# Remainders of up to 64 rows of a routed layer, multiplied two experts at a time

## The chip, the core and the metric

The kernel runs on one core of one Trainium2 chip. The core has TensorE (PE in the profile, its weight loads PEld), VectorE (DVE), ScalarE (ACT), GpSimd (POOL) and SyncE (SP, which here mainly issues transfers), each with its own instruction stream, and 16 DMA engines that all queues share. The metric is the device time of one execution in microseconds (us). One profiled execution, with a record of every instruction, stands beside the timed runs.

## The reference, cut to what matters

Four layers follow each other, each added to `x` (3125 rows of 256): an attention over a graph, a layer of 16 experts of which each row uses two, a sum over the graph, and a layer of 8 experts of which each row uses one. The change is in the last one:

```python
H = gelu(xf @ W1 + b1, approximate=False)          # 3125 x 1024
probs = softmax((H @ Wg + bg) / TEMP, axis=-1)     # 3125 x 8
assign = argmax(probs, axis=-1)
for e in range(8):
    y = H @ Wd[e] + bd[e]                          # Wd[e]: 1024 x 256
    out = out + where((assign == e)[:, None], probs[:, e:e + 1] * y, 0.0)
x = x + out
```

Only the product with the chosen expert's `Wd[e]` is needed for a row. Which rows choose which expert is known only when the kernel runs.

## The kernel before, in words

The last layer is `routed_top1`. Its first part goes through the nodes in chunks of 512: hidden values `H`, the gate's product, the choice, and for every row its place among the rows of its expert. Each row (1024 hidden values, 256 values of `x`, its number and its probability, 1282 floats in all) is written to the DRAM table `rows` by an indirect transfer, the rows of expert `e` one behind another from `e * 3200` on. A matrix product then gives `total`, the rows of each expert.

From `total` some twenty small VectorE operations on a single partition make the `table` of slots. A slot is 128 rows of one expert. `table[0]` holds the slot's expert and `table[1]` its first row in `rows`. An expert with n rows has ceil(n / 128) slots; its last slot can be nearly empty. All weights `Wd` were loaded into `t_wd` (`d` in the code) before, 8 copies of 1 MB (line 1600). While the table is made, `keep_warm` lets TensorE run matmuls whose results nobody reads (line 558).

The second part, `slots`, runs 30 slots (`USUAL`), one after another, for all inputs. If there are more (`rest` is 1), the conditional part at the end runs those up to `SLOTS` with fewer buffers. One slot is:

- SP reads the expert and the first row from `table` and issues the copy of 128 rows into `hs` (641 KB, line 1044) and of the expert's bias (line 1046). There are four buffers of `hs`, so the rows of slot s wait until slot s-4 has been finished by VectorE.
- TensorE turns the 128 x 1024 hidden values in eight transposes (`ps_cols`, line 1051), ScalarE copies them to `hsT` (line 1052).
- TensorE reads the expert from `table` too, and multiplies (`multiply`, `ps_y`, line 1024): eight products of 128 x 128 by 128 x 256, each of two instructions in float32. The product of a slot comes after the transposes of the next.
- VectorE adds the bias (line 1027), scales and adds `x` (line 1028) and converts the row numbers (`who`, line 1031). POOL writes the rows of `out` with an indirect transfer (line 1032).

A scheduler sets the order of the instructions on each engine within what the data allow. On SP the order is that of the program in this part.

With the reference's inputs the eight experts have 525, 260, 708, 139, 167, 442, 490 and 394 rows.

Two places outside this part matter below. Each layer of the graph keeps its data in two large blocks of the pool `big`; none is read any more once the first part of `routed_top1` is over. And the layer of 16 experts already multiplies remainders of up to 64 rows in pairs: `first_more` and `second_more` hold the rows of one expert in the lower and of another in the upper half of a tile, fetch both experts' weights (line 817), and multiply each half with its own:

```python
for j in range(nh):
    for half, _, _, o in own:
        nc.tensor.matmul(ps[half], hid[:, j, half], o[:, j], start=(j == 0), stop=(j == nh - 1))   # line 847
```

Of the kernel before, what the change touches and what calls it, by code (L numbers as in the profile page):

```python
# [10 lines left out]
F32 = mybir.dt.float32  # L11
F16 = mybir.dt.float16
BF16 = mybir.dt.bfloat16
I32 = mybir.dt.int32
# [3 lines left out]
OP = mybir.AluOpType  # L18
AX = mybir.AxisListType
# [3 lines left out]
P = 128  # L23
N = 3125
NT = 25
LAST = N - (NT - 1) * P
NP = NT * P
D = 256
# [9 lines left out]
NX0, HID0 = 16, 512  # L38
NX1, HID1 = 8, 1024
# [484 lines left out]
SHARE = P // 2  # L524
SUBS = NX0 * (CAP0 - EACH * P) // SHARE
BETWEEN = 5
CAP1 = 1024
SLOTS = (N + NX1 * (P - 1)) // P
USUAL = 30
ROW0 = D + 2  # L530
ROW1 = HID1 + D + 2
QUAD = 32
# [350 lines left out]
            nc.sync.dma_start(x[:, t:t + n], sums[t * P:(t + n) * P].rearrange("(t p) f -> p t f", p=P))  # L883


def routed_top1(tc, x, xnT, ident, iota, count, weights, rows, out, over):

# [1 line left out]

    nc = tc.nc
    before, every = count
    (a, b1, (g, fold), gb), (d, bd) = weights
    nh = HID1 // P
    with tc.tile_pool(name="u1", bufs=1) as cp:
        first = cp.tile([P, NX1], F32, name="first")
# [8 lines left out]
                                channel_multiplier=-1)  # L906
# [3 lines left out]
        pre = cp.tile([P, NT + 1, NX1], BF16, name="pre")  # L910
        nc.vector.memset(pre[:, 0], 0.0)
        table = cp.tile([1, 2, SLOTS], I32, name="table")
        warm = cp.tile([P, P], F32, name="warm")
        nc.gpsimd.memset(warm, 0.0)
        rest = cp.tile([1, 1], I32, name="rest")
        end = cp.tile([1, 4, 2 * NX1], F32, name="end")
        nc.vector.memset(end, 0.0)
        with tc.tile_pool(name="uh", bufs=2) as hp, tc.tile_pool(name="uw", bufs=2) as wp, \
             tc.tile_pool(name="ur", bufs=6) as rp, \
             tc.tile_pool(name="uph", bufs=2, space=PSUM) as pp, \  # L920
# [66 lines left out]
            keep_warm(nc, tp.tile([P, CHUNK], F32, name="ps_rows"), warm, d[:, 0, 0:2].rearrange("p j f -> p (j f)"), 8)  # L987
            nc.vector.tensor_reduce(over, total, AX.X, OP.max)
            ni = cp.tile([1, NX1], I32, name="n_i")
            nc.vector.tensor_scalar(ni, total, float(P - 1), None, op0=OP.add)  # L990
            nc.vector.tensor_scalar(ni, ni, 7, None, op0=OP.arith_shift_right)

            nc.vector.tensor_copy(end[:, 0, NX1:], ni)
            for j in range(3):
                nc.vector.tensor_tensor(end[:, j + 1, NX1:], end[:, j, NX1:], end[:, j, NX1 - (1 << j):-(1 << j)],
                                        op=OP.add)
            end = end[:, 3, NX1:]
            nc.vector.tensor_scalar(rest, end[:, NX1 - 1:], float(USUAL), None, op0=OP.is_gt)
            slot = cp.tile([1, SLOTS], F32, name="slot")
            nc.gpsimd.iota(slot, pattern=[[1, SLOTS]], base=0, channel_multiplier=0,  # L1000
                           allow_small_or_imprecise_dtypes=True)
# [13 lines left out]

            nc.vector.tensor_scalar(table[:, 1], slot, float(NX1 * NT), float(P), op0=OP.min, op1=OP.mult)

        def slots(which, pools):
            xp, sp, tp, po = pools

            def multiply(hs, hsT, bias, e):
                ps = po.tile([P, D], F32, name="ps_y")
                for j in range(nh):
                    nc.tensor.matmul(ps, hsT[:, j], d[:, ds(e, 1), j, :].rearrange("p o f -> p (o f)"),  # L1024
                                     start=(j == 0), stop=(j == nh - 1))
                y = sp.tile([P, D], F32, name="y")
                nc.vector.tensor_tensor(bias, ps, bias, op=OP.add)
                nc.vector.scalar_tensor_tensor(y, bias, hs[:, HID1 + D + 1:], hs[:, HID1:HID1 + D], op0=OP.mult,
                                               op1=OP.add)
                who = sp.tile([P, 1], I32, name="who")  # L1030
                nc.vector.tensor_copy(who, hs[:, HID1 + D:HID1 + D + 1])
                independent(tc, "out", nc.gpsimd.indirect_dma_start(
                    out=out, out_offset=bass.IndirectOffsetOnAxis(ap=who, axis=0), in_=y, in_offset=None,
                    bounds_check=N - 1, oob_is_err=False))

            ready = None
            for s in which:
                e = nc.values_load(table[0:1, 0, s:s + 1], engines=(mybir.EngineType.PE, mybir.EngineType.SP), min_val=0,
                                   max_val=NX1 - 1, skip_runtime_bounds_check_because="min with the last expert")
                at = nc.values_load(table[0:1, 1, s:s + 1], engines=(mybir.EngineType.SP,), min_val=0,  # L1040
                                    max_val=NX1 * NP, skip_runtime_bounds_check_because="min with the spare tile")
                hs = xp.tile([P, ROW1], F32, name="hs")
                for c, n in ((0, ROW1),) if s else ((0, HID1 // 2), (HID1 // 2, ROW1 - HID1 // 2)):
                    nc.sync.dma_start(hs[:, c:c + n], rows[ds(at, P), c:c + n])
                bias = xp.tile([P, D], F32, name="bias")
                nc.sync.dma_start(bias, bd[ds(e, 1), :].to_broadcast([P, D]))
                hsT = xp.tile([P, nh, P], F32, name="hsT")
                for h in range(0, nh, 4):
                    ps = tp.tile([P, 4, P], F32, name="ps_cols")
                    for j in range(4):  # L1050
                        nc.tensor.transpose(ps[:, j], hs[:, (h + j) * P:(h + j + 1) * P], ident)  # L1051
                    nc.scalar.copy(hsT[:, h:h + 4], ps)  # L1052
                if ready:
                    multiply(*ready)
                ready = hs, hsT, bias, e
            multiply(*ready)

        def pools(stack, bufs):
            return [stack.enter_context(tc.tile_pool(name=name, bufs=b, **kw)) for name, b, kw in (
                ("vx", min(4, bufs), {}), ("vs", bufs, {}), ("vpt", min(4, bufs), dict(space=PSUM)),  # L1060
                ("vpo", min(3, bufs), dict(space=PSUM)))]

        with ExitStack() as stack:
            slots(range(USUAL), pools(stack, 6))
        more = nc.values_load(rest[0:1, 0:1], min_val=0, max_val=1, skip_runtime_bounds_check_because="0 or 1")
        with tc.If(more > 0), ExitStack() as stack:
            slots(range(USUAL, SLOTS), pools(stack, 2))

# [62 lines left out]
def block(big, d=D):  # L1133

    return big.tile([P, NT * ROW], F32, name="big")[:, :NT * d].rearrange("p (t d) -> p t d", d=d)
# [459 lines left out]


def output_weights(nc, cp, wd, bd):
    d = cp.tile([P, NX1, HID1 // P, D], F32, name="t_wd")
    for e in range(NX1):
        nc.sync.dma_start(d[:, e], wd[e].rearrange("(k p) f -> p k f", p=P))  # L1600
    return d, bd


WIN = 5
# [406 lines left out]
@with_exitstack  # L2011
def routed(ctx: ExitStack, tc: tile.TileContext, i: dict, out: bass.AP, over):
    nc = tc.nc
    const = ctx.enter_context(tc.tile_pool(name="const", bufs=1))
    dram = ctx.enter_context(tc.tile_pool(name="dram", bufs=1, space=DRAM))
    ident, eps, iota = constants(tc, const)
    count = counters(tc, const)
    rows0 = dram.tile([NX0 * NP + P, ROW0], F32, name="rows0")
    rows = dram.tile([NX1 * NP + P, ROW1], F32, name="rows1")
    sums = dram.tile([NP + CAP0, D], F32, name="sums0")  # L2020
    layers = [[i[f"L0_gnn_{n}{j}"] for n in ("W", "al", "ar", "b")] for j in (1, 2, 3)]
    big = ctx.enter_context(tc.tile_pool(name="big", bufs=2))
    early = ctx.enter_context(tc.tile_pool(name="early", bufs=1))
    more = early.tile([1, 3, SUBS], I32, name="more")
    with tc.tile_pool(name="counts", bufs=1) as kp:
        counts = kp.tile([P, NT * ((len(GROUPS) - 1) * PAIR + 64)], U8, name="counts")
        x = dense_attention(tc, dram, counts, i["x"], big, ident, eps, layers, i["src"], i["dst"], (rows0, rows),
                            over[:, 3:4], lambda cp: Router(tc, cp, ident, eps, iota, count, rows0, sums,
                                                            i["L0_ffn_gate_w"], i["L0_ffn_gate_b"], more), over[:, 0:1], count)
        with tc.tile_pool(name="s0", bufs=1) as sp:  # L2030
            ws, wm = (sp.tile([P, KD, D], F32, name="s_" + n) for n in "WM")
            hidden = hidden_weights(nc, early, *(i["L1_ffn_" + n] for n in ("W1", "b1", "Wg", "bg")), x[:, 0, 0:1])
            room = block(big).rearrange("p t d -> p (t d)")
            xnT = room.rearrange("p (k n) -> p k n", k=KD)
            routed_experts(tc, x, room, ident, rows0, sums, more, *(i["L0_ffn_" + n] for n in ("w1", "w2", "w3")),
                           lambda behind: [two_halves(nc, to, i["L1_gnn_" + n], behind) for to, n in ((ws, "W"), (wm, "M"))])
            dense_sum(tc, x, xnT, counts, ws, wm, ident, eps, over[:, 2:3])
    late = ctx.enter_context(tc.tile_pool(name="late", bufs=1))
    weights = hidden, output_weights(nc, late, *(i["L1_ffn_" + n] for n in ("Wd", "bd")))
    routed_top1(tc, x, xnT, ident, iota[:, NX0 - NX1:], count, weights, rows, out, over[:, 1:2])  # L2040


def load_nodes(nc, x, x_in, first=0, end=NT):
# [88 lines left out]
```

## Time and profile before

| | |
|---|---|
| three timed runs | 1888.25, 1891.96, 1897.26 us (median 1891.96) |
| the profiled execution | 1840.01 us |
| its span, first to last instruction | 1838.2 us |
| first part of `routed_top1` | from 1551 to 1686 us |
| table and warming matmuls | from 1686 to 1696 us |
| slots | from 1696 to 1829 us |
| rows of a slot (`hs`, 641 KB), issue to landing | 2.6 / 4.3 / 6.5 us (least / median / most) |
| bias of a slot (128 KB), issue to landing | 3.3 / 4.0 / 7.1 us |
| resident `Wd` (1 MB each, 8 in a row), issue to landing | 5.7 / 10.7 / 12.2 us |

The profile has a page and further views. The page gives each engine's busy time and what share of the span that is. The windows give, for a stretch of time, the busy time of each engine with the number of its instructions, the clock granted to TensorE (1.00 is full), the mean busy share of the DMA engines and the rate in GB/s. The timeline lists single instructions or runs of equal ones, with start and duration; at the end of a line, in brackets, stands how long the engine was idle and what ended it. The chain of waits goes back from the last instruction to what released each, and lists its pieces in order of time. "L1044" is line 1044 of the kernel.

### The profile page before, as it was taken

The page shows a single profiled execution, that of the slowest core. Times are in us where ns is not written, and L with a number is a line of the kernel's source. Part 1 is how long each engine was busy: PE and PEld are TensorE (multiplying, and loading weights), DVE is VectorE, ACT ScalarE, POOL GpSimd, SP SyncE. Part 2 cuts the span into 40 slices and gives each one's busy share as a digit, 9 for nine tenths or more (in the row PEclk, how much of TensorE's full clock was granted, in tenths as well). Part 3 has the DMA queues.
Part 4 walks back from the last instruction along what each step waited for, and adds up shares of the span by engine and source line. Part 5 has one row for each costly group of instructions (what it writes and reads, how often), then busy time and mean ns, then how long its engine had stood idle before and what let it go on. Part 6 is the DMA issues. An engine that isn't in the chain of part 4 may idle for free. (4 is left out here: it accounts for less than half of the span.)

```text
span 1838.2 us, 27323 instructions
## 1 busy us (share of the span) xinstructions
PE 1771.2 (96%) x9249; PEld 1389.5 (76%) x9249; DVE 1017.4 (55%) x2865; ACT 725.4 (39%) x2078; POOL 501.5 (27%) x636
## 2 busy tenths in 40 slices
PE   5999999999999999999999799999989999999997
PEld 4788888887887886888888466666668886555886
DVE  6888888875777887777777422222262222233221
ACT  3767667671111111222222211111148998444221
POOL 5210110000677774223322233333200000222221
PEclk9999999999999999999999899999999999999999
DMA  4111213757333332211111576776330002624664
GB/s 118 33 48 47 67 64 139 298 236 312 80 93 95 98 93 78 62 46 40 40 44 37 178 196 196 204 217 168 66 82 1 1 1 74 225 115 166 215 203 127
DMA packets 118370, 211.50 MB, mean 115 GB/s; under 512 B 14843, under 2 KB 80929, under 8 KB 118184
## 3 DMA queue, kind: packets, MB, share of 16 engines
q1 hardware_dynamic: 78228, 130.30, 20.9%
q0 software_dynamic: 24848, 56.84, 11.8%
q10 hardware_dynamic: 15138, 22.44, 3.7%
q8 instruction: 79, 1.29, 0.3%
q14 instruction: 77, 0.63, 0.1%
HBM read 118.61 MB, written 93.00 MB: 115 GB/s over the span
## 5 line engine op out<-in xcount | busy, mean ns | idle before, releaser
L1391 PE MATMUL acc<-big,pm 128*128 128x257 f32 x3400 | 787.7, 383 | 8.9 <-DVE pm L1388 8.9
L1391 PEld LDWEIGHTS acc<-big,pm 128*128 128x128 f32 x3400 | 628.6, 190 | 99.4 <-DVE pm L1388 15.4
L1388 DVE SCALAR_TENSOR_TENSOR pm<-tau,big,counts 128x256 f32<-128x256 f32 x850 | 398.3, 487 | 99.9 <-PE acc L1391 96.0
L1933 POOL DMA_INDIRECT apart_row<-apart_rows,apart_who x172 | 186.7, 1085 | 62.6 <-issue 39.3
L775 PE MATMUL ps_h<-xsT,w 128*128 128x384 f32 x512 | 168.4, 487 | 0.6 <-ACT xsT L751 0.6
L1543 PE MATMUL acc<-msg,cr 128*128 128x512 f32 (+1 forms) x625 | 157.9, 403 | 0.0
L775 PEld LDWEIGHTS ps_h<-xsT,w 128*128 128x128 f32 x512 | 96.7, 190 | 66.9 <-issue 1.9
L1543 PEld LDWEIGHTS acc<-msg,cr 128*128 128x128 f32 (+1 forms) x625 | 114.7, 185 | 29.2 <-ACT cr L1539 1.2
L1539 ACT ACTIVATE cr<-counts 128x256 fp32r<-128x256 uint8 (+1 forms) x325 | 130.6, 402 | 14.2 <-PE acc L1543 7.0
L1799 ACT CAST counts<-acc_c 128x500 uint8<-128x500 f32 (+1 forms) x155 | 95.9, 677 | 94.8 <-PE acc_c L1789 94.7
L1024 PE MATMUL ps_y<-t_wd,hsT 128*128 x480 | 108.8, 380 | 0.4 <-ACT hsT L1052 0.4
L1774 DVE TENSOR_TENSOR ohk<-iota_k,key 128x2016 f16<-128x2016 f16 (+1 forms) x79 | 94.6, 1197 | 19.8 <-PE acc_c L1789 19.7
L778 ACT ACTIVATE silu<-ps_h 128x384 f32<-128x384 f32 x64 | 31.4, 490 | 182.2 <-PE ps_h L775 182.1
L795 POOL DMA_INDIRECT sums<-y,who x48 | 74.7, 1556 | 85.9 <-DVE y L793 73.0
L1024 PEld LDWEIGHTS ps_y<-t_wd,hsT 128*128 128x128 f32 x480 | 88.8, 190 | 11.6 <-ACT hsT L1052 0.6
L779 DVE TENSOR_TENSOR hid<-silu,ps_h 128x384 f32<-128x384 f32 x64 | 35.2, 553 | 108.7 <-PE ps_h L775 103.9
L1768 ACT ACTIVATE ohs<-iota_s,low 128x128 f16<-128x128 f16 x286 | 94.1, 400 | 0.0
L930 PE MATMUL ps_H<-big,t_w 128*128 128x512 f32 (+1 forms) x224 | 93.1, 552 | 0.8 <-ACT H L932 0.5
L790 PE MATMUL ps_o<-w,hid 128*128 128x256 f32 x384 | 87.2, 379 | 0.0
L1789 PEld LDWEIGHTS <-ohs 128*128 128x128 f16 x1250 | 77.7, 98 | 10.9
L1789 PE MATMUL acc_c<-ohk,ohs 128*128 128x125 f16 x1250 | 84.5, 218 | 0.0
L1959 DVE SCALAR_TENSOR_TENSOR apart_acc<-apart_row,apart_co,apart_acc 128x257 f32<-128x257 f32 x167 | 80.9, 485 | 1.6
(380 smaller groups left out, 2073.5 us busy)
## 6 DMA issues: line engine op xcount, KB each, us to landing
rows<-empty SPq DMA_DIRECT2D x16, 2564.0 KB, 15.7
w<-in_L_ffn_w_dram ACTq DMA_DIRECT2D x42, 512.0 KB, 4.9
hs<-rows SPq DMA_DIRECT2D x29, 641.0 KB, 4.4
big<-in_L_ffn_w_dram SPq DMA_DIRECT2D x30, 512.0 KB, 9.2
rows<-empty SPq DMA_DIRECT2D x16, 516.0 KB, 4.8
t_wd<-in_L_ffn_Wd_dram SPq DMA_DIRECT2D x8, 1024.0 KB, 10.7
xs<-rows SPq DMA_DIRECT2D x15, 387.0 KB, 3.4
bias<-in_L_ffn_bd_dram SPq DMA_DIRECT2D x30, 128.0 KB, 4.0
```

The costliest lines, as they stand in the source:

```text
L775: nc.tensor.matmul(ps, w[:, k, j * P:(j + 1) * P], xsT[:, k], start=(k == 0), stop=(k == KD - 1))
L930: nc.tensor.matmul(ps[:, :n], a[:, k, j * P:(j + 1) * P], xnT[:, k, c:c + n], start=(k == 0), stop=(k == KD - 1))
L1024: nc.tensor.matmul(ps, hsT[:, j], d[:, ds(e, 1), j, :].rearrange("p o f -> p (o f)"), start=(j == 0), stop=(j == nh - 1))
L1388: nc.vector.scalar_tensor_tensor(pm[:, :n], tau[:, :n], now.rho[:, of:of + 1], edges[:, of, :n], op0=OP.max, op1=OP.mult)
L1391: nc.tensor.matmul(acc[:r, j, :D + 1], pm[:, q:q + r], now.h[:, of, :D + 1], start=(s == 0), stop=(s == NT - 1))
L1539: nc.scalar.activation(cr[:, :n], edges[:, s, :n], AF.Copy, accum_out=seen[:, a * NT + s:a * NT + s + 1])
L1543: nc.tensor.matmul(acc[:r, j].rearrange("p h d -> p (h d)"), cr[:, q:q + r], msg[:, s].rearrange("p h d -> p (h d)"), start=(s == 0), stop ...
L1768: nc.scalar.activation(far[:, i], self.iota_s, AF.Abs, scale=-1.0, bias=self.low32[:, batch, i:i + 1])
L1774: nc.vector.tensor_tensor(to[:, i:tiles].rearrange("p t (x u) -> p t x u", u=2), iota.rearrange("p (x u) -> p x u", u=2)[:, None].to_broad ...
L1789: nc.tensor.matmul(acc[:, u], ohs[:, i], ohk[:, i, :KEYS], start=(t == 0), stop=(t == TW - 1))
L1799: nc.scalar.copy(to[:, :, d0 % PAIR:d0 % PAIR + whole * WIN].rearrange("p s (u d) -> p u s d", u=whole), acc[:, :whole])
L1933: nc.gpsimd.indirect_dma_start(out=row[:, j], out_offset=None, in_=self.table[:, :], in_offset=bass.IndirectOffsetOnAxis(ap=self.who[:, q ...
```

## The change

An expert's last rows no longer fill a slot of 128 if they are 64 or fewer. They become a half. Full slots are now floor((n + 63) / 128) for n rows; an expert with rows beyond these has one half. Two halves, of two experts, make a pair: their rows lie in the lower and the upper 64 partitions of one `hs`, and each half is multiplied with its own expert's weights, 64 rows wide, into its half of one PSUM tile.

24 slots and 3 pairs run for all inputs; 4 more slots and one pair are in the conditional part, which runs if there are more than 24 full slots or more than 6 halves. The table of slots has 28 columns instead of 32. A second table, `ends` (named `ends_table`), holds expert and first row of each half, and is made by further small operations on VectorE.

The pairs come after the slots. Their weights aren't taken from `t_wd`, but fetched from DRAM into two blocks of `big` (three halves of 1 MB in each); TensorE then needs no expert number for them. The fetches are issued on SP, one ahead of the rows of every second slot from slot 6 (`LATER`) on: at slots 6, 8, 10, 12, 14 and 16.

The core of the diff:

```diff
-SLOTS = (N + NX1 * (P - 1)) // P
-USUAL = 30
+SLOTS = (N + NX1 * (P - SHARE - 1)) // P
+USUAL = 24
+PAIRS = NX1 // 2
+USUAL_PAIRS = 3
+LATER = 6
...
-            nc.vector.tensor_scalar(ni, total, float(P - 1), None, op0=OP.add)
+            nc.vector.tensor_scalar(ni, total, float(P - SHARE - 1), None, op0=OP.add)
             nc.vector.tensor_scalar(ni, ni, 7, None, op0=OP.arith_shift_right)
...
+            own = cp.tile([1, NX1], F32, name="own_half")
+            nc.vector.scalar_tensor_tensor(own, whole, float(P), total, op0=OP.mult, op1=OP.is_lt)
+            nc.vector.tensor_copy(last[:, 0, NX1:], own)
...
+            nc.vector.tensor_scalar(many[:, 0:1], end[:, NX1 - 1:], float(USUAL), None, op0=OP.is_gt)
+            nc.vector.tensor_scalar(many[:, 1:2], last[:, NX1 - 1:], float(2 * USUAL_PAIRS), None, op0=OP.is_gt)
+            nc.vector.tensor_tensor(rest, many[:, 0:1], many[:, 1:2], op=OP.max)
...
+        blocks = [block(big, ROW).rearrange("p t d -> p (t d)") for _ in range(2)]
...
                 for j in range(nh):
-                    nc.tensor.matmul(ps, hsT[:, j], d[:, ds(e, 1), j, :].rearrange("p o f -> p (o f)"),
-                                     start=(j == 0), stop=(j == nh - 1))
+                    for part, of in own:
+                        nc.tensor.matmul(ps[part], hsT[:, j, part], of(j), start=(j == 0), stop=(j == nh - 1))
...
+            def halves(k):
+                e = nc.values_load(ends[0:1, 0, k:k + 1], engines=(mybir.EngineType.SP,), min_val=0,
+                                   max_val=NX1 - 1, skip_runtime_bounds_check_because="min with the last expert")
+                to = blocks[k // 3 % 2][:, k % 3 * nh * D:(k % 3 + 1) * nh * D].rearrange("p (j f) -> p j f", f=D)
+                nc.sync.dma_start(to, wd[ds(e, 1)].rearrange("o (k p) f -> p (o k) f", p=P))
+                return e, to
...
+            for s, of, parts in [(s, table, [whole]) for s in which] + \
+                    [(2 * s, ends, [slice(0, SHARE), slice(SHARE, P)]) for s in pairs]:
                 hs = xp.tile([P, ROW1], F32, name="hs")
...
+                soon = [k for k in range(2 * pairs[0], 2 * pairs[-1] + 2) if k not in loaded]
+                if of is table and s >= LATER and s % 2 == 0 and soon:
+                    loaded[soon[0]] = halves(soon[0])
+                for k, part in enumerate(parts):
...
+                    for c, n in ((0, ROW1),) if s or of is ends else ((0, HID1 // 2), (HID1 // 2, ROW1 - HID1 // 2)):
+                        nc.sync.dma_start(hs[part, c:c + n], rows[ds(at, rs), c:c + n])
+                    nc.sync.dma_start(bias[part], bd[ds(e, 1), :].to_broadcast([rs, D]))
...
-            slots(range(USUAL), pools(stack, 6))
+            slots(range(USUAL), range(USUAL_PAIRS), pools(stack, 6))
...
-            slots(range(USUAL, SLOTS), pools(stack, 2))
+            slots(range(USUAL, SLOTS), range(USUAL_PAIRS, PAIRS), pools(stack, 2))
```

## The prediction

> **What bounds the kernel now.** I read the busy shares and the 40 slices first, then the windows of the last stage, then the chain of waits, then single rows. The page says where the end is set:
>
> ```profile
> PE 1771.2 (96%) x9249; PEld 1389.5 (76%) x9249; DVE 1017.4 (55%) x2865; ACT 725.4 (39%) x2078; POOL 501.5 (27%) x636
> ```
>
> TensorE is busy 96% of the span. A share is an average, so the stage of the change, the output slots, is read alone. It runs from 1696 us to 1829 us (busy time of the engines, granted clock, DMA share, GB/s):
>
> ```profile
> 1700.00:1740.00 40.00, 40.00 (x227) 35.76 (x226) 9.50 (x28) 10.74 (x20) 8.80 (x9) 1.00 0.67 210
> 1740.00:1780.00 40.00, 40.00 (x223) 35.71 (x222) 9.57 (x27) 9.66 (x18) 8.78 (x9) 1.00 0.68 212
> ```
>
> TensorE has no gap here and full clock. Every other engine is under a quarter busy, apart from the weight loads, which run beside the matmuls. The chain of waits gives the beat of a slot:
>
> ```profile
> 1724.51 0.87 PE ps_cols L1051 x8
> 1725.39 3.46 PE ps_y L1024 x16
> 1728.84 0.87 PE ps_cols L1051 x8
> ```
>
> A slot is 0.87 us of transposes and 3.46 us of multiplication, 4.33 us from slot to slot. Nothing else is in the chain, so a slot less is 4.33 us less, as long as rows and weights keep coming in time.
>
> **How many slots go.** The gate of the reference, evaluated on its own inputs, sends 525, 260, 708, 139, 167, 442, 490 and 394 rows to the eight experts. Rounded up to 128 these are 5+3+6+2+2+4+4+4 = 30 slots, all that the kernel before runs. After the change a remainder of up to 64 is a half: 13, 4, 11, 39, 58 and 10 are (experts 0, 1, 3, 4, 5, 7), 68 and 106 are not. So 24 full slots and 6 halves, which is exactly 24 slots and 3 pairs. The flag `rest` stays 0 and the conditional slots are jumped over.
>
> **Removed.** Six slots at 4.33 us: -26.0 us of TensorE time on the path.
>
> **Added on TensorE: three pairs.** A pair has the same 8 transposes (0.87 us) and twice as many matmuls: for each of 8 blocks one with the 64 rows of one half and one with those of the other, each streaming 256 columns. The stage has no such row, but an earlier one of this trace does: line 847 multiplies two halves of 64 rows into the two halves of one PSUM tile in the same way, also with 256 columns. Timeline of that place (start, duration):
>
> ```profile
> 1110.25 1.89 PE L790 MATMUL ps_o<-w,hid 128*128 128x256 f32 x8
> 1112.07 1.95 PE L847 MATMUL ps_o<-big,silu 128*64 128x256 f32 x16
> 1113.95 0.59 PE L775 MATMUL ps_h<-xsT,w 128*128 128x384 f32 x1
> ```
>
> Eight full-width instructions took 1.82 us from start to start, the sixteen half-width ones 1.88 us. Two halves run side by side for the price of one. At 3.46/16 = 0.216 us, eight instructions are 1.73 us, so going into the half-width form cost 0.09 us and coming out 0.15 us. In the changed program the 96 half-width matmul instructions of the pairs stand in three runs, parted by transposes: three entries and two exits before the end, 0.6 us. Three pairs: 3 x 4.33 + 0.6 = +13.6 us.
>
> A rule of the Trainium skill speaks against this. TensorE: Matmul & The Clock Gate, Part 3, "The mechanism", says that a weight load overlaps a running matmul only where the row groups differ, and both halves here use all 128 rows. By the rule each couple would pay two loads (0.137 us each, median of line 847) and 0.216 us of streaming: 0.49 us, 16 couples 7.8 us, three pairs 3 x (0.87 + 7.8) = 26.1 us, and the change would gain nothing (-26.0 + 26.1). The rows disagree: 16 loads of 137 ns, 2.2 us in all, went by within 1.88 us that also held their matmuls. I take the row.
>
> **Added on SP: the fetched weights.** Six copies of 1 MB of `Wd` into free blocks of `big`, one ahead of the rows of slots 6, 8, 10, 12, 14 and 16, each with a load of its expert number from `ends`. SP needs about 0.7 us for that: 0.38 us to issue (median of line 817, the same kind of copy) and 0.3 us for the number. Before the stage settles SP passes a slot in 1.66 us (issues of `hs` at 1694.17 and 1695.83); afterwards it waits for a free row buffer, so 0.7 us vanishes in the wait. Behind SP stand the rows `hs` and the bias of the next slot. What can hurt is the transfer:
>
> ```profile
> 1703.98 0.33 SPq L1044 DMA_DIRECT2D hs<-rows  x1
> 1708.17 0.15 DVE L1031 CAST who<-hs 128x1 int32<-128x1 f32 x1
> 1711.15 0.90 PEld L1051 LDWEIGHTS ps_cols<-ident,hs 128*128 128x128 f32 x7
> ```
>
> The rows of slot 4 are issued at 1703.98, their first reader `who` has them at 1708.17, and TensorE takes them at 1711.15: 7.2 us from issue to need, 4.2 us used, 3.0 us to spare. The fetch of the resident weights shows the full rate (same columns as above):
>
> ```profile
> 1556.00:1561.00 5.00, 4.82 (x12) 2.20 (x12) 0.00 (x0) 2.41 (x5) 0.00 (x0) 1.00 1.09 354
> 1561.00:1566.00 5.00, 5.00 (x13) 2.28 (x12) 0.00 (x0) 2.06 (x3) 0.00 (x0) 1.00 1.09 348
> ```
>
> At 350 GB/s 1 MB takes 3.0 us. Two slots now move 8.66 us x 211 GB/s = 1.83 MB; with 1.05 MB more it is 333 GB/s, 95% of the full rate, for the 12 slots that fetch. That fits, with little left. My estimate of the landing: the copy is issued some 2.4 us before the next rows, so about 1.5 us of it is still ahead of them: 4.2 + 1.5 = 5.7 us of the 7.2. The rule that speaks against it is in DMA: Bandwidth & Descriptors, "Queues, rings and completion order": descriptors of one issuing queue are consumed in ring order on each engine. If none of the copy had moved when the rows are issued, they would land after 4.2 + 3.0 = 7.2 us, just in time; with the bias and output rows of a slot before them (0.26 MB, 0.75 us) 0.75 us late, six times, 4.5 us. From the row 0, from the rule 4.5 us at worst. I take 0.3 us and keep 0 to 4.5 for the range.
>
> In the pairs SP issues four copies instead of two, with two loads of a number: the second half's rows go out about 1.4 us after the first's, hence wanted within 5.8 us and landing in 4.2. Hidden by the same spare time; without it each pair would lose what is missing.
>
> **Added on VectorE and POOL.** Some 20 small operations on one partition, 0.13 to 0.2 us each, and one more iota. About 12 of them stand among those that make `table`, on which the first rows wait (table ready 1690.65, first rows issued 1691.79). Dependent operations there start 0.2 us apart, independent ones 0.07 us, so most fill gaps, and the tables shrink from 32 to 28 columns. Worked along the new order, `table` is 0 to 0.3 us later. The warming matmuls hold TensorE to 1696.36, but the rows of slot 2 arrive at 1702.34 and are read at 1702.49, so a delay shows almost whole. I take +0.2 us (-0.2 to +0.7). The rest, done about 2 us later, is over before the first `who` at 1695.73; were it not, `who` and the output rows would wait, not TensorE. ScalarE loses six copies of 0.59 us and gains none on the path.
>
> **Unchanged.** After the last matmul: add, scale, output row copy, drain, as before (9.4 us from 1828.80). Ahead of 1686 us only two clears of small tiles are new. The longer jumped-over part costs 0, at most 0.5 us either way.
>
> **Sum.** -26.0 + 13.6 + 0.3 + 0.2 = -11.9 us. The profiled execution took 1840.01 us (span 1838.2 and 1.8 around it), so it would take 1828.1 us. The runs shown have a median of 1891.96 us, 52 us above the profiled one; the profile does not say where that lies. I take the difference over in microseconds: 1891.96 - 11.9 = 1880.1 us. Scaled with the time it would be -12.2.
>
> **The rivals.**
>
> *The fetch starves the slots (gain halved or gone).* The rows of slots 6 to 17 come late because the DMA engines run at 95%. For: 512 KB copies from line 817 took 9.0 us to land while another queue also fetched, and `hs` took up to 6.5 us. Against: 3.0 us to spare, and only every second slot has a fetch before it. In the chain, transfers of `hs` would appear in this stretch. At 0.75 us a fetch it is -7.7 us (1884); at 2 us a fetch the gain is gone (1892). Chance 0.2 for a loss of 3 us or more.
>
> *The halves do not run side by side,* the rule above or plain one-after-the-other: three pairs of 0.87 + 32 x 0.216 = 7.8 us, 23.4 us, -2.6 us before the other costs and about -2 after: 1890. Only line 847 speaks on it, and against. Chance 0.04.
>
> *The conditional part runs (slower).* The 24 slots and 3 pairs fit without any spare: one half more, or one full slot more, sets `rest`, and then 4 slots and a pair run with two row buffers. Rows are then issued only when the slot two before is done: 0.95 us of VectorE, 4.2 us of landing, 0.87 and 3.46 us of TensorE, 9.5 us each, 47 us for five, and about 10 us to start (a 1 MB fetch, then rows). 1880 + 57 = 1937. It decides at the 25th full slot or the 7th half; nearest is expert 2, whose 68 must fall to 64. Four rows of 3125 would have to choose otherwise than in the reference. Chance 0.04.
>
> **How the numbers follow.** The forecast (loss to the fetch under 3 us) has 0.72. A measurement of this kernel can tell about 0.5%, 9.5 us, from no change, so 1882.5 is the border, only 2.4 us above the forecast. With the runs shown spreading from -3.7 to +5.3 us about their median, the forecast lies beyond the border in some six cases of seven: 0.62; the starving case adds 0.02. Slower: the conditional part 0.04, a bad fetch or a shifted median 0.02. Within 0.5%: the remaining 0.30. The range: below, the best of the unknowns (no loss to fetch and table, clean halves) gives 1879, less the spread and something for scaling, 1871; above, the starving case with its gain gone, 1892.
>
> **What would show it.** In the profile after: 384 instructions of `ps_y` from `t_wd` and 96 of 128*64 from `big`; about 117 us from the first `ps_cols` to the last `ps_y` in place of 130; `hs` landing at 5 to 6 us behind a fetch and TensorE without gap; the sixteen couples of a pair in about 3.5 us. Wrong are: waits of `ps_cols` for `hs`, DMA rows in the chain between slots 6 and 17, a pair above 5 us, or any slot at the conditional lines.

## The result, and the profile after

| | before | after |
|---|---|---|
| median of 6 runs | 1892.12 us (1886.5 to 1899.18) | 1878.69 us (1872.85 to 1885.01) |
| profiled execution | 1840.01 us | 1872.85 us |
| its span | 1838.2 us | 1871.1 us |
| slots and pairs: first `ps_cols` to start of the last bias addition | 130.8 us | 119.4 us |
| last `place` (start of the work on the table) to start of the last bias addition | 141.7 us | 130.0 us |

The ratio is 0.9931 (95% interval 0.9905 to 0.9958): 13.4 us less, or 8 to 18 us by the interval. The forecast was 11.9 us less, 1880.1 us. Line numbers after are shifted: the transposes `ps_cols` are L1111, the multiplication `ps_y` L1064, the issue of rows L1105, of fetched weights L1079, `who` L1070, the bias addition L1066; in experiments 9 and 10 they are one or two higher.

The two profiles look as if the kernel had become 33 us slower. That is the trap of this case, and the windows of the two profiles show where it lies: in the attention, over 900 us ahead of the change. First before, then after (busy times of the engines, granted clock, DMA share, GB/s):

```profile
440.00:800.00 360.00, 348.63 (x1672) 289.40 (x1671) 267.51 (x757) 55.87 (x178) 207.91 (x223) 1.00 0.33 95
```

```profile
440.00:800.00 360.00, 314.93 (x1452) 255.90 (x1451) 232.81 (x637) 45.94 (x158) 190.28 (x196) 0.95 0.30 87
```

In the same 360 us, 1452 matmuls were done instead of 1672, although the change leaves that part of the program alone. The profile of the kernel before is of none of the timed runs in the table: at 1840.01 us it lies 46 us below the fastest of them. Experiment 8 shows that the 45 us by which the slots begin later (1742 instead of 1697 us) go with the comparison, not with the change. So the stages are compared by their own length. Here is the stage of the change, after:

```profile
1742.00:1762.00 20.00, 19.64 (x114) 17.43 (x113) 4.23 (x14) 6.20 (x12) 3.04 (x4) 1.00 0.83 252
1762.00:1782.00 20.00, 19.71 (x108) 17.32 (x107) 4.21 (x12) 4.55 (x9) 4.80 (x5) 1.00 1.02 341
1782.00:1802.00 20.00, 20.00 (x110) 17.84 (x109) 5.00 (x15) 4.30 (x8) 4.56 (x5) 1.00 0.94 328
...
1822.00:1842.00 20.00, 20.00 (x113) 17.89 (x112) 4.78 (x14) 5.37 (x10) 4.89 (x5) 1.00 0.67 203
```

While the weights are fetched, the transfers rise to 341 GB/s (the forecast said 333), and TensorE is short by 0.3 us in that window. Afterwards the rate falls to 203 GB/s, near the 210 of the kernel before. TensorE remains the bound.

The gap stands in the timeline (start, duration, idle time before it and what ended it):

```profile
1755.50 0.38 SPq L1079 DMA_DIRECT2D big<-in_L_ffn_Wd_dram  x1
...
1758.66 0.33 SPq L1105 DMA_DIRECT2D hs<-rows  x1
...
1760.48 1.04 PE L1111 MATMUL ps_cols<-ident,hs 128*128 128x128 f32 x8
...
1765.22 0.15 DVE L1070 CAST who<-hs 128x1 int32<-128x1 f32 x1 [3.59 <-DMA hs<-rows]
...
1765.27 1.06 PE L1111 MATMUL ps_cols<-ident,hs 128*128 128x128 f32 x8 [0.29 <-DMA hs<-rows]
...
1773.68 0.15 DVE L1070 CAST who<-hs 128x1 int32<-128x1 f32 x1 [2.91 <-DMA hs<-rows]
```

The rows of slot 6 are issued 3.2 us after the first fetch and land after 6.5 us. The transposes start at 1765.27, 4.79 us after those of slot 5 (1760.48) where the beat is 4.33: a gap of 0.46 us, and the only one of this kind in this profile.

The rows of slot 8, behind the second fetch, are issued at 1766.40 and land at 1773.68, after 7.3 us. Their transposes start at 1773.95, so only 0.27 us was to spare. In a third profile of the changed kernel (experiment 12) these rows land after 8.6 us, and TensorE waits:

```profile
1728.53 1.06 PE L1111 MATMUL ps_cols<-ident,hs 128*128 128x128 f32 x8 [0.95 <-DMA hs<-rows]
```

That gap is 1.12 us against the beat. With the 0.48 us of slot 6 the fetches cost 1.6 us there, and 0.5 us in the second profile (experiment 8).

Why no gap comes after slot 8, though later rows land no sooner, is in the chain of waits (start, length, what):

```profile
1774.99 3.46 PE ps_y L1064 x16
1778.44 0.87 PE ps_cols L1111 x8
1779.32 5.61 PE ps_y L1064 x26
1784.93 0.87 PE ps_cols L1111 x8
1785.81 1.30 PE ps_y L1064 x6
1787.10 0.87 PE ps_cols L1111 x8
1787.98 6.05 PE ps_y L1064 x28
```

From here on TensorE's order isn't 8 transposes and 16 matmuls by turns any more. Ahead of some transposes 26 or 28 matmuls stand, 2.2 to 2.6 us more than 16, and ahead of the next only 6 or 4. The scheduler placed the transposes of the even slots from 10 on later in the program, those behind a fetch, so their rows have that much longer to land. In the third profile this decided: the rows of slot 14 landed at 1756.44, after 9.2 us. By turns of 8 and 16 their transposes would have been due at 1754.53, and in the new order they started at 1757.12, without a wait.

And the three pairs, timeline of TensorE:

```profile
1847.64 2.37 PE L1064 MATMUL ps_y<-big,hsT 128*64 128x256 f32 x18
...
1849.94 1.09 PE L1111 MATMUL ps_cols<-ident,hs 128*128 128x128 f32 x8
...
1850.97 4.11 PE L1064 MATMUL ps_y<-big,hsT 128*64 128x256 f32 x36
...
1855.01 1.09 PE L1111 MATMUL ps_cols<-ident,hs 128*128 128x128 f32 x8
...
1856.03 4.96 PE L1064 MATMUL ps_y<-big,hsT 128*64 128x256 f32 x42
```

36 half-width instructions take 4.04 us from their start to the transposes, 0.112 us each: side by side, as in line 847. The transposes between two runs take 1.02 us from start to start instead of 0.87.

### The profile page after: what moved, and what is told of

It reads as the page before. It is cut to its first block, busy times and chain, and to the rows that moved or that the text cites. A ratio compares the mean times of both kernels' runs of the same rounds, so it can differ in the third digit from the quotient of the medians.

```text
span 1871.1 us, 27222 instructions
## 1 busy us (share of the span) xinstructions
PE 1769.9 (95%) x9225; PEld 1380.9 (74%) x9225; DVE 1015.9 (54%) x2875; ACT 723.7 (39%) x2072; POOL 494.1 (26%) x634
## 3 DMA queue, kind: packets, MB, share of 16 engines
q0 software_dynamic: 24704, 56.84, 11.3%
## 5 line engine op out<-in xcount | busy, mean ns | idle before, releaser
L1994 POOL DMA_INDIRECT apart_row<-apart_rows,apart_who x172 | 182.5, 1061 | 99.4 <-issue 43.5
L1599 ACT ACTIVATE cr<-counts 128x256 fp32r<-128x256 uint8 (+1 forms) x325 | 130.8, 403 | 14.2 <-PE acc L1603 7.0
L781 ACT ACTIVATE silu<-ps_h 128x384 f32<-128x384 f32 x64 | 31.5, 492 | 182.1 <-PE ps_h L778 177.9
L1221 PE MATMUL ps_m<-we,yT 128*128 128x258 f32 (+1 forms) x248 | 72.1, 411 | 21.1 <-ACT yT L1351 16.9
L1351 ACT ACTIVATE yT<-ps_m 128x256 f32<-128x256 f32 (+1 forms) x25 | 9.5, 380 | 210.3 <-PE ps_m L1349 145.2
L1064 PE MATMUL ps_y<-t_wd,hsT 128*128 x384 | 87.1, 379 | 0.4 <-ACT hsT L1112 0.4
```

The lines of the kernel that those rows point to most:

```text
L1064: nc.tensor.matmul(ps[part], hsT[:, j, part], of(j), start=(j == 0), stop=(j == nh - 1))
L1599: nc.scalar.activation(cr[:, :n], edges[:, s, :n], AF.Copy, accum_out=seen[:, a * NT + s:a * NT + s + 1])
L1994: nc.gpsimd.indirect_dma_start(out=row[:, j], out_offset=None, in_=self.table[:, :], in_offset=bass.IndirectOffsetOnAxis(ap=self.who[:, q ...
```

## The experiments

Each comparison ran on one chip, and the chips differed: the kernel before took 1838 to 1839 us on three of them (experiments 1 to 8, 11 and 12) and 1896 us on one (experiments 9 and 10). Each ratio is against the kernel before in the same comparison. A "stage" below is the time from the first `ps_cols` to the start of the last bias addition. When the first transposes start early, TensorE waits a microsecond or more for the rows of slots 0 and 1; that wait is part of a stage, so stages are comparable only to about that much.

**1. The kernel before, profiled again.**

> The kernel before, profiled once more. The two profiles on hand start their slots at 1697 us (before) and 1742 us (after), although no instruction ahead of 1686 us differs but for two clears. Theory (the 45 us are a difference between executions, not of the change): this profile lies anywhere between 1840 and 1897 us, with the slots still taking 131 us from the first transpose to the last bias addition (130.8 us in the first profile) whatever the stages ahead take. Rival (the change makes the earlier stages slower by about 45 us and the slots gain as much elsewhere): the slots start again within 3 us of 1697 us.

It took 1837.15 us, where the kernel before had a median of 1838.31 us (24 runs), and its stage took 130.9 us. The slots started at 1694 us, so this run alone fits the letter of the rival: it met no slow attention. What it settles is that the stage is steady: 130.8 and 130.9 us. The 45 us are decided by experiment 8.

**2. Six slots left out.**

> The kernel before with 24 slots in place of 30; the rows of the last six slots are left out. Theory (TensorE alone sets the pace of the slots, 4.33 us each): 26.0 us less than before, 1866 us by the medians, ratio 0.9863, so that the three pairs of the change cost the remaining 26.0 - 13.4 = about 12.6 us. Rival (rows, output transfers or a fixed end set part of the stage): 13 us less or under, as much as the changed kernel.

```diff
-            slots(range(USUAL), pools(stack, 6))
+            slots(range(USUAL - 6), pools(stack, 6))
```

1812.64 against 1838.31 us: 25.7 us less, ratio 0.9862 (0.9839 to 0.9885). The slots are on the path at full length. Its stage is 105.8 us, 25.0 less, and 1.6 us of that went to waits for rows at its start, so the stage's length has an uncertainty of a microsecond or two at its head. Of the 25.7 us the change gains 13.2 in experiments 8 and 12, so the three pairs, their fetches and the longer table cost about 12.5 us together.

**3. One half after the other.**

> The changed kernel, but each pair multiplies all eight blocks of one half and then all eight of the other, so that neighbouring matmuls fill the same 64 columns of TensorE. Theory (two halves run side by side only because neighbours use different columns): a matmul instruction of a pair costs 0.216 us again, 32 of them 6.9 us in place of 3.5: 3 x 3.46 = 10.4 us above the changed kernel, 1889 us, and almost nothing gained on before. Rival (the short weight load of 64 columns makes the half-width form cheap by itself): no change from the changed kernel, 1879 us.

```diff
-                for j in range(nh):
-                    for part, of in own:
+                for part, of in own:
+                    for j in range(nh):
```

1833.63 us, ratio 0.998 (0.997 to 0.999); the changed kernel, on another chip on which the kernel before takes 1838 us, lies at 1825.10 us (experiment 8). So it is 8.5 us slower than that, where 10.4 had been expected; the stage is 125.4 us, 6.0 longer than 119.4. The rival, which saw no change, is out. But the size was off. Timeline:

```profile
1802.07 2.80 PE L1064 MATMUL ps_y<-big,hsT 128*64 128x256 f32 x12
1804.81 1.09 PE L1111 MATMUL ps_cols<-ident,hs 128*128 128x128 f32 x8
1805.83 5.46 PE L1064 MATMUL ps_y<-big,hsT 128*64 128x256 f32 x32
```

The run of 12 holds one half only and costs 2.74/12 = 0.23 us each, as one after the other must. The run of 32, with two changes of half in it, costs 5.40/32 = 0.169. Windows of 0.4 us within that run (the first count is of the `ps_y` matmuls in flight):

```profile
1806.20:1806.60 0.40, 0.40 (x8) 0.26 (x5) 0.00 (x0) 1.00 0.00 0
...
1807.40:1807.80 0.40, 0.40 (x3) 0.27 (x2) 0.00 (x0) 1.00 0.00 0
...
1808.60:1809.00 0.40, 0.40 (x7) 0.36 (x7) 0.00 (x0) 1.00 0.00 0
```

Two bursts of 7 to 8, and 3 between them. I read this so: where the half changes, a few matmuls of the new half run beside the last of the old one. Experiment 10 tests that.

**4. No fetch.**

> The changed kernel without the six fetches: the pairs take their weights from the resident copy, at experts 0, 1, 3, 4, 5 and 7 written into the program, which are those of these inputs. Theory (the fetch is hidden but for the gap ahead of the transposes of slot 6, 0.3 to 0.5 us): 0.5 us below the changed kernel, not to be told from it in time; in the profile that gap is gone and the rows land in 4 to 5 us throughout. Rival (the fetch slows the slots by several us): 3 us below it or more, 1875 us.

```diff
-                        e, to = loaded.get(s + k) or halves(s + k)
-                        own.append((part, lambda j, to=to: to[:, j]))
+                        e = nc.values_load(of[0:1, 0, s + k:s + k + 1], engines=(mybir.EngineType.SP,), min_val=0,
+                                           max_val=NX1 - 1, ...)
+                        own.append((part, lambda j, c=(0, 1, 3, 4, 5, 7, 7, 7)[s + k]: d[:, c, j]))
```

The early `halves` in the loop is gone too. The kernel took 1828.04 us, ratio 0.9939 (0.992 to 0.9959), against 0.9931 with the fetches: nothing won in time. In its windows TensorE has no gap, at 223 GB/s instead of 341:

```profile
1715.00:1755.00 40.00, 40.00 (x225) 35.72 (x224) 9.75 (x28) 9.66 (x18) 8.79 (x9) 1.00 0.71 223
```

Its stage is 118.8 us, 0.6 below the first profile of the changed kernel and 1.7 below the two later ones. From the last `place` to the last bias addition it is 129.8 us, against 130.0, 130.0 and 131.4. So the six megabytes of transfers cost 0.3 to 1.7 us, as the gaps above say. Rows landed after 4.2 us (median), 6.0 at most.

**5. A fetch ahead of every slot.**

> The changed kernel with the six fetches ahead of six slots in a row (6 to 11) instead of every second one. Theory (the fetch is free only as long as the DMA engines keep up): a slot and a fetch move 0.92 + 1.05 = 1.97 MB, 5.6 us at 350 GB/s against the slot's 4.33; six slots come 7.7 us behind, of which some 2 to 3 us of spare time take part: TensorE waits 4 to 6 us for rows in slots 6 to 13, and the kernel is 4 to 6 us slower than the changed one. Rival (the queue is not near its limit, the one gap at slot 6 is the start of the fetching): one gap of 0.5 us again, the time of the changed kernel.

```diff
-                if of is table and s >= LATER and s % 2 == 0 and soon:
+                if of is table and s >= LATER and soon:
```

1830.56 us, ratio 0.9964 (0.9951 to 0.9976): 5.5 us above the changed kernel. As the theory had it, the spacing of the fetches is what keeps them cheap. Window and SP's timeline:

```profile
1720.00:1740.00 20.00, 19.16 (x103) 16.44 (x102) 4.94 (x14) 4.23 (x8) 4.18 (x5) 1.00 1.07 376
```

```profile
1726.91 2.25 SPq L1105 DMA_DIRECT2D hs<-rows  x1
...
1731.44 2.78 SPq L1105 DMA_DIRECT2D hs<-rows  x1
```

The DMA share is 1.07 (1.09 in the fetch of `t_wd`), rows land after up to 11.3 us, and the issue of a copy, 0.33 us otherwise, holds SP for 2 to 3 us. The waits of TensorE and of its weight loads for rows are 2.7 us, and the stage grew to 123.0 us, 2.5 to 3.6 above the changed kernel's. That accounts for the profiled execution, which was the fastest of the eleven: 1826.33 us, 2.3 above the profile of experiment 8. The other runs took up to 1836.69 us, and what they lost beyond that isn't shown.

**6. `who` on POOL.**

> The changed kernel with the conversion of the row numbers, who, on POOL instead of VectorE. In the chain of the changed kernel who of a coming slot stands in VectorE's order ahead of y of a past one; who waits for its rows to land, y waits for who, and the next rows wait for y, which frees their buffer. Theory (this loop makes the gap ahead of slot 6): rows are issued 0.5 us after the bias addition throughout, TensorE's gap at slot 6 is gone, 0.5 us less, not to be told in time. Rival (the rows of slot 6 are late only because they queue behind the first fetch): the gap stays at 0.4 to 0.5 us. Third way (POOL's small copies delay its output transfers): the end is 0.5 us later.

```diff
-                nc.vector.tensor_copy(who, hs[:, HID1 + D:HID1 + D + 1])
+                nc.gpsimd.tensor_copy(who, hs[:, HID1 + D:HID1 + D + 1])
```

1827.40 us, ratio 0.9946 (0.993 to 0.9963), not to be told from the changed kernel. The timeline speaks for the rival (rows of slot 6 issued, and their transposes):

```profile
1709.73 0.33 SPq L1105 DMA_DIRECT2D hs<-rows  x1
...
1717.39 1.06 PE L1111 MATMUL ps_cols<-ident,hs 128*128 128x128 f32 x8 [0.18 <-DMA hs<-rows]
```

The rows of slot 6 now go out at once after `y`, and still TensorE gets them only 7.7 us later, with 0.34 us lost against the beat. Without the fetch the gap is gone (experiment 4), so the fetch ahead of these rows makes it. The loop over `who` is real in the chain, but it isn't needed for the gap.

**7. The conditional part, made to run.**

> The changed kernel with the flag set at 24 full slots instead of above 24, so that the conditional part runs for these inputs: four slots and one pair, all beyond the rows there are, whose results go nowhere. This prices the case in which an input has one half or one full slot too many. Theory (two row buffers let nothing run ahead): 9.5 us for each of five and about 10 us to start, 47 + 10 = 57 us above the changed kernel. Rival (the conditional part overlaps nearly as well as the main one): five times 4.33 and one landing of 5 us, about 27 us.

```diff
-            nc.vector.tensor_scalar(many[:, 0:1], end[:, NX1 - 1:], float(USUAL), None, op0=OP.is_gt)
+            nc.vector.tensor_scalar(many[:, 0:1], end[:, NX1 - 1:], float(USUAL - 1), None, op0=OP.is_gt)
```

1869.69 us, ratio 1.0183 (1.0162 to 1.0205): 44.6 us above the changed kernel, between the two expectations. SP's and TensorE's timelines:

```profile
1813.10 0.33 SPq L1105 DMA_DIRECT2D hs<-rows  x1
...
1814.77 0.33 SPq L1105 DMA_DIRECT2D hs<-rows  x1
...
1827.93 0.33 SPq L1105 DMA_DIRECT2D hs<-rows  x1
```

```profile
1822.52 7.75 PE L1064 MATMUL ps_y<-t_wd,hsT 128*128 x30
```

The rows of two slots go out 1.7 us apart, and those of the next two only when a buffer comes free, at 1827.93 and 1831.38, so two slots share most of one landing. Against that, 30 matmuls take 7.75 us, 0.26 each instead of 0.216; the clock granted between 1811 and 1831 us was 0.74, where the stage ran at 1.00. The kernel is 31.5 us slower here than the kernel before. About that much is the price where the conditional part runs after the change and not before: 23 full slots and 7 halves are still 30 slots for the kernel before. That is the case that the forecast named, four rows fewer for expert 2. With 31 tiles or more the kernel before runs its conditional part as well, and what that costs was not measured.

**8. The changed kernel again.**

> The changed kernel once more, on a chip where the kernel before takes 1838 us instead of 1892. Theory (the change takes a fixed amount of TensorE time out of the slots, whatever the stages ahead take): 11 to 13 us below before, ratio 0.9931 again within 0.002, and the slots last 119 us from the first transpose to the last bias addition, as in the first profile of the changed kernel (119.4), while the 45 us that profile lost in the attention (480 to 760 us) are not there. Rival (part of the gain belongs to the other chip): ratio 0.996 or above.

1825.10 against 1838.23 us, ratio 0.9931 (0.9914 to 0.9947). The gain is the same 13 us on another chip, and the attention is fast there with the changed kernel too:

```profile
440.00:800.00 360.00, 351.52 (x1687) 292.40 (x1685) 270.69 (x767) 57.73 (x181) 205.80 (x224) 1.00 0.33 95
```

It has 1687 matmuls, about as many as the profile of the kernel before (1672). So the 45 us don't belong to the change. The stage took 120.5 us, with some 1 us of waiting for the rows and bias of slots 0 and 1 that the first profile had not. From the last `place` to the last bias addition it is 130.0 us, as in the first profile.

**9. Four remainders in one tile.** The kernel of experiment 4 with its six halves laid out as one tile of four and one pair:

> The kernel without fetches, with one step more: the four remainders of up to 32 rows (13, 4, 11 and 10, experts 0, 1, 3 and 7) share one 128-row tile, each 32 rows wide in its own 32 columns of TensorE, and the two others (39 and 58, experts 4 and 5) make one pair. Experts and places are written into the program for these inputs. Theory (column groups run side by side, four as well as two): the four products of a block cost one streaming, 0.216 us per instruction group, so the tile costs about 4.6 us and the stage falls by one pair's 4.7 us against the kernel without fetches, from 118.8 to about 114.2 us. Rival (the weight loads set a floor: sixteen of 64 columns went by in 1.5 us, 0.093 us each): 64 loads and matmuls of the tile take at least 5.9 us in place of 3.5, and the stage falls by only 2 us.

```diff
+MIXED = [(0, [(0, slice(0, 32)), (1, slice(32, 64)), (2, slice(64, 96)), (5, slice(96, 128))]),
+         (0, [(3, slice(0, 64)), (4, slice(64, 128))])]
...
-                    [(2 * s, ends, [slice(0, SHARE), slice(SHARE, P)]) for s in pairs]:
+                    [(s, ends, parts) for s, parts in MIXED if pairs[0] == 0]:
```

```profile
1849.70 3.64 PE L1066 MATMUL ps_y<-t_wd,hsT 128*32 128x256 f32 x58 [0.29 <-ACT hsT L1114]
1853.28 1.09 PE L1113 MATMUL ps_cols<-ident,hs 128*128 128x128 f32 x8
```

58 instructions of 32 columns take 3.58 us, 0.062 us each: four side by side, and below the floor of 0.093 us that the rival took from the weight loads. The stage fell to 114.8 us, 4.0 below experiment 4. The time, 0.9929 (0.9906 to 0.9952), could not show so little on this chip, where the runs scatter by 17 us.

**10. Halves alternating every four blocks.**

> The changed kernel with the halves of a pair alternating every four blocks (eight instructions) instead of every block; the kernel with halves one after the other alternated every eight. That one cost 0.169 us an instruction, neither the 0.216 of one after the other nor the 0.11 of side by side. Theory (about four instructions at each change of half run beside those before the change, the rest wait for their own columns): three changes within a pair instead of one, 2 x 3 more, each saving about 0.8 us: some 4 us less than with halves one after the other, the stage at 121 to 122 us instead of 125.4. Rival (an instruction of 64 columns costs 0.169 us whenever its neighbours use the same columns): no change, 125 us.

```diff
-                for j in range(nh):
-                    for part, of in own:
-                        nc.tensor.matmul(ps[part], hsT[:, j, part], of(j), start=(j == 0), stop=(j == nh - 1))
+                for j0 in range(0, nh, 4):
+                    for part, of in own:
+                        for j in range(j0, j0 + 4):
+                            nc.tensor.matmul(ps[part], hsT[:, j, part], of(j), start=(j == 0), stop=(j == nh - 1))
```

```profile
1868.15 4.33 PE L1065 MATMUL ps_y<-big,hsT 128*64 128x256 f32 x34
```

34 instructions in 4.25 us, 0.125 each: between 0.112 and 0.169, as the number of changes would have it. The stage took 121.8 us, with 1.2 us of waiting for rows. The time (0.9955, 0.9933 to 0.9978) says nothing finer. The distance can be estimated from these numbers. A run of 16 instructions in the same columns takes 16 x 0.169 = 2.7 us, the time of 12 at the 0.23 us of an instruction alone; a run of 8 takes 1.0 us, the time of 4 to 5. So about four instructions at each change run beside those of the other half. The order within a pair decides how much of that is used.

**11 and 12. Four in a tile beside the changed kernel.**

> The kernel with one tile of four remainders and one pair again (experts and places written into the program for these inputs), now timed in more rounds beside the changed kernel on the same chip. In the profiles its slots took 114.8 us against 119.3 and 120.5 of the changed kernel. Theory (the stage is on the path as a whole): 4 to 6 us below the changed kernel, 16 to 18 us below before, ratio about 0.991. Rival (something after the slots takes it back): the ratio of the changed kernel, 0.993.

> The changed kernel beside it, for the comparison: 12 to 13 us below before, ratio 0.993 as in both comparisons so far.

Before 1838.86 us; with four in a tile 1821.25 us, ratio 0.9911 (0.9895 to 0.9927); the changed kernel 1825.69 us, ratio 0.9928 (0.9914 to 0.9941). That is 17.6 us gained in place of 13.2. The difference of 4.4 us is about a pair's, but the two intervals overlap, and the kernel also does without the fetches. The profile agrees: from the last `place` to the last bias addition it is 126.4 us with four in a tile and 131.4 us for the changed kernel beside it. (The stage as counted above is 117.5 us, not 114.8 as in experiment 9, for TensorE waited 3.1 us for the first rows.) As built it holds for these inputs alone; a kernel for all inputs would need a third table and places for the case in which fewer than four remainders are that small.

## Why the prediction was right, point by point

- **TensorE sets the pace, 4.33 us a slot.** Right: six slots are worth 25.7 us in the timed runs (26.0 forecast). One reading was off without harm: ScalarE, at 10.74 of 40 us in the first window, was 27% busy and not under a quarter.
- **A pair costs a slot, 13.6 us for three.** Right in kind, short in size by the profile: 0.87 us for the first transposes, then 13.4 us from the first half-width matmul to the last bias addition, less the 0.2 us that an addition starts after the end of the chain's matmul, 14.1 us. Beyond three times 4.33 that is 1.1 us, where the forecast carried over 0.6 from line 847 for going into the half-width form and out of it. Part of it is in the transposes that follow a half-width run: 0.15 us more for each of two. The 12.5 us that the timed runs leave for pairs, fetches and table (experiment 2) can't decide between 13.6 and 14.1: the interval of each ratio in it is 3 to 4 us wide to either side.
- **Weight loads.** The Trainium skill's rule (TensorE: Matmul & The Clock Gate, Part 3, "The mechanism") would have made a pair 8.7 us. The pairs took 4.7, and with four in a tile 58 loads went by in 3.58 us. For halves that share all rows and fill different columns, this kernel shows the loads overlapping. The plain slots had spoken against so strict a reading already: their loads, too, use all 128 rows, and in the first window of the forecast they are busy for 35.76 of 40 us in which TensorE has no gap. The same section also lets a load run ahead into a background weight buffer, which the forecast left out; no run here shows which way these loads took.
- **Side by side.** The rival of halves one after the other is refuted by experiment 3: without the alternation 8.5 of the 13.2 us are gone. Experiment 10 lies between, as the number of changes would have it.
- **The fetch.** It cost 0.5 us in two profiles and 1.6 in the third, where 0.3 had been taken. The landing was estimated at 5.7 us; it was 6.5 for slot 6, and up to 9.2 in the third profile. The estimate of 7.2 us from the second rule of the Trainium skill, ring order (DMA: Bandwidth & Descriptors, "Queues, rings and completion order"), was nearer: the rows of slot 8 took 7.3 us in two profiles and 8.6 in the third. The runs show only the landing, not the order within a ring. At slot 8 it was close, by 0.27 us. From slot 10 on the later place of the transposes gave the rows more time, and that the forecast did not foresee: here it was lucky. The starving rival exists, but needs a fetch at every slot (experiment 5: 5.5 us).
- **The table.** From `place` to `table` it is 4.62 us before and 4.82 after, +0.2 as forecast. It cost nothing: from `place` to the fifth transposes it is 25.5 and 25.6 us before, 25.1 to 25.4 after.
- **The conditional part.** It didn't run. Its price of 57 us was too high; 44.6 was measured, because two slots share most of one landing.
- **The signs.** The 384 and 96 matmuls of `ps_y` are there. From the first `ps_cols` to the last `ps_y` it is 130.4 us before and 118.9 after; the forecast said about 117, though its own sum gives 118.5. One sign of being wrong came, but small: `ps_cols` waited for `hs`.
- **Where the number was lucky.** The kernel lost 13.1 to 13.4 us, 1.2 to 1.5 more than forecast, although the pairs and the fetches cost more than forecast. From the last `place` to the last bias addition three profiles of the changed kernel lost 11.7, 11.7 and 10.3 us against the first of the kernel before; the sum of the forecast, 11.9, belongs to that stretch. (The length is good to about a microsecond: in experiment 2 it fell by 27.3 us, the time by 25.7.) Behind it lies half a microsecond (10.6 us to the end before, 10.1 after). The rest, about a microsecond, lies ahead of that point, which the profiles on the three faster chips reach between 1680.9 and 1685.9 us. Against such a scatter it can't be given to the change.

## What to carry to other kernels

Small products that use only half or a quarter of TensorE's columns are worth pairing when they can be issued by turns. Lay the loop so that neighbours fill different columns, since here only some four instructions at each change ran together. When they need other weights, fetch these at a rate that the stage's own transfers leave free, and look at the order of the consumer as well as at the landing: six fetches of a megabyte cost 0.5 to 1.6 us here at one for every 8.7 us, and made the kernel another 5.5 us slower at one for every 4.3 us.

Compare a changed stage with itself before you look at the span: the two profiles differ by 33 us in the wrong direction, and the cause lay over 900 us earlier in code that had not changed. Choose the start of such a stage with care, too: the first transposes can begin early and then wait, so a start in the part that did not change (`place` here) is the fairer one.

## What the runs showed of the hardware that was not expected

- The same program takes 1838 us on some chips and 1892 to 1896 us on others. The difference lies between 440 and 800 us, where POOL gathers rows one after another. In that stretch all profiles of the faster chips have 1684 to 1702 matmuls, the profile of 1840 us 1672, and those of the slower chips 1452, 1456 and 1404 (the first of the changed kernel, and experiments 9 and 10). In the first of these TensorE and VectorE stand idle together at times, as for over 6 us at 491 us, while POOL goes on. Each chip was used once, so chip and moment can't be told apart, and the cause isn't shown.
- Four instructions of 32 columns take little longer than one of 128: 4 x 0.062 = 0.25 us against 0.216.
- Between full overlap (0.112 us) and none (0.23 us) there are steps in between, set by how often neighbours change their columns: 0.125 and 0.169 us.
